# Where ScalarE copies a list's own mask: ahead of the list's other columns, or behind its last evacuation

## The chip, the cores and the metric

The kernel runs on one core of a Trainium2 chip. The metric is the device time of one execution in microseconds (us); where several executions were timed, the median is given. Lower is better.

## The reference, cut to what matters

Four graph attention layers on 4096 nodes with 256 features, each with a residual and a layer norm. All four use one adjacency matrix, which is about 1/256 full and has its diagonal set:

```python
x = layernorm(x + gat0(x, adj, ...))     # 4 heads of 64
x = layernorm(x + gat1(x, adj, ...))     # 4 heads of 64
x = layernorm(x + gat2(x, adj, ...))     # 2 heads of 128
x = layernorm(x + gat3(x, adj, ...))     # 1 head of 256, a positive and a negative softmax
# in each layer, for node i and neighbour j:
#   e_ij = leaky_relu(s_i + d_j, 0.2), -inf where adj_ij is 0
#   out_i = sum_j softmax_j(e_ij) * v_j
```

## The kernel before, in words

**Lists.** The 4096 nodes are 32 row tiles of 128. A row tile of 128 nodes has neighbours in about 40% of all nodes, so the kernel does not run over all columns. For each row tile it packs a *list*: 14 groups of 128 columns each (`NP = 14`), of which 13 are gathered neighbours and one, at place `FRONT = 6`, is the row tile itself. A list has two products. One is the packed mask, `cm`, of 128 x 14 x 132 bytes: for each packed column, 128 mask bytes and four bytes with the digits of the column's node number. It is stored to `maskC` in HBM. The other is the table `idx` of node numbers, which is worked out from the digits and stays on the chip. All four layers read both.

**How a list is made** (`lists`, L288). Four row tiles make a block. For a block, `prepare` (L370) loads raw adjacency (L378, four buffers `raw`), has ScalarE convert it to mask bytes `mk` (L380), and VectorE reduces it to which columns are hit (L384). `places` (L389) works out where each hit column goes in the list. `pack` (L422) then makes one list: VectorE builds one-hot matrices `oh` (L436), TensorE multiplies them with `mk` into PSUM banks (L442), and ScalarE evacuates each full bank into `cm` (L449, five evacuations per list: four of three groups, one of one group). The group `FRONT` needs no matmul: ScalarE copies it from `mk` (L425). When `cm` is whole, SyncE issues its store (L450), and three small VectorE operations make the index table from it (L453 to L455). The pool of `cm` has three buffers (L297), so a list's buffer is the one that the list three before used.

**The layers.** In a layer, each row tile gathers its 13 groups of node rows with indirect DMAs on GpSimd (L634), and loads its own rows (L631), its packed mask (L626) and a row of scores (L624) through SyncE. ScalarE computes weights (L687, 42 per row tile in layer 0), VectorE more weights and the masking (L678, L682, L684, L688), and TensorE multiplies weights and gathered rows (L696). Row tiles are done in two halves of seven groups. The result is normalised on VectorE (L1014 to L1017, L967 to L988), and projected for the next layer: L536 transposes, L541 copies, L550 multiplies, L568 and L574 (ScalarE) with L570 and L576 (VectorE) make the row that L578 stores. L588 and L589 make and store the scores.

**What runs beside what** (`run`, L482). Layer 0 begins before the lists are done. The first ten to fourteen lists are made while layer 0's projections run (up to about 160 us). From then on one list and one conversion step are made between the two halves of each row tile of layer 0, ten row tiles ahead (`LEAD = 10`). The last list is stored at 664 us. From there on layers 0 to 3 run alone. (A dense path behind the packed one runs only where a list overflows, which this input doesn't cause.)

**What sets the order.** The program gives instructions in the order of the code, but a scheduler places them in each engine's queue by its own estimate of when they can start. An engine works through its queue in order. So an instruction that depends on little can be placed a long way ahead of its neighbours in the code; its waits are then met where it stands in the queue. L425 depends on `mk`, which is there for a whole block at a time, and on its buffer.

Of the kernel before, what the change touches and what calls it, by code (L numbers as in the profile page):

```python
# [44 lines left out]
AF = mybir.ActivationFunctionType  # L45
# [33 lines left out]
FRONT = 6  # L79
# [3 lines left out]
EDGE = 64.0  # L83
# [105 lines left out]
class Program:  # L189
# [98 lines left out]
    def lists(self, ctx):  # L288


        tc, nc, ins, shared = self.tc, self.nc, self.ins, self.shared
# [52 lines left out]
        for j in range(NT):  # L344
            m = 0
            while m < NT:
# [3 lines left out]
                e = m  # L350
# [5 lines left out]
                m = e  # L356
# [7 lines left out]
        class Block:  # L364
# [57 lines left out]
            def pack(self, it):  # L422
                m, mk = self.blk * BT + it, self.mk
                cm = cmp_.tile([P, NP, MC], U8, name="cm")
                nc.scalar.copy(cm[:, FRONT, :], mk[:, m, it, :])  # L425
                order = [j for j in range(NT) if j != m]
                touches = {}
                for j in order:
                    a, n = WINDOW[m, j]
                    for k in range(a, a + n):  # L430
                        touches.setdefault(k // 3, []).append((j, k))
                accs = {}
                for j in order:
                    a, n = WINDOW[m, j]
                    oh = ohp.tile([P, WMAX], BF16, name="oh")
                    nc.vector.tensor_scalar(oh[:, :n * P], iota[:, :n * P], self.place[:, it, j:j + 1], None,  # L436
                                            op0=ALU.is_equal)
                    for k in range(a, a + n):
                        b, s = divmod(k, 3)
                        if b not in accs:  # L440
                            accs[b] = prog.bank(prog.pthree)
                        nc.tensor.matmul(accs[b][:, s * MC:(s + 1) * MC], oh[:, (k - a) * P:(k - a + 1) * P],  # L442
                                         mk[:, j, it, :].bitcast(FP8), start=touches[b][0] == (j, k),
                                         stop=touches[b][-1] == (j, k), skip_group_check=True)
                        if touches[b][-1] == (j, k):
                            e = min(3, NG - 3 * b)
                            got = accs[b][:, :e * MC].rearrange("p (s c) -> p s c", c=MC)
                            o = 3 * b + (3 * b >= FRONT)
                            nc.scalar.activation(cm[:, o:o + e, :], got, AF.Copy, scale=EDGE / 2.0)  # L449
                nc.sync.dma_start(out=shared["maskC"][m], in_=cm)  # L450

                t = wk.tile([P, NP], F32, name="t")
                nc.vector.scalar_tensor_tensor(t, cm[:, :, P], 16.0, cm[:, :, P + 1], op0=ALU.mult, op1=ALU.add)  # L453
                nc.vector.scalar_tensor_tensor(t, t, 16.0, cm[:, :, P + 2], op0=ALU.mult, op1=ALU.add)
                nc.vector.tensor_tensor(shared["idx"][:, m, :], t, limit, op=ALU.min)  # L455
# [1034 lines left out]
```

## Time and profile before

| | before |
|---|---|
| median of 3 runs | 2287.78 us (2284.84 to 2289.15) |
| the profiled execution | 2288.18 us, span 2286.40 us |
| busy: TensorE, weight load | 2026.1 us, 1835.8 us |
| busy: VectorE, ScalarE, GpSimd | 1798.3 us, 1741.5 us, 1493.2 us |
| mean granted TensorE clock | 0.961 |
| list copies L425 | 32 of 0.30 us |
| list evacuations L449 | 160, mostly of 0.50 us |
| stores of `cm` L450 | 32, the first at 66.3 us, the last at 664.2 us |

Times in the profile count from the start of the span. "L425" is line 425 of the kernel before. In a view of the chain of work or of waits, a piece such as "DMA maskC<-cm" is the time from the issue of a store to its landing, for which the next piece waited. In a view by stretches, "busy" counts an engine's instructions only, so a stretch's length less an engine's busy time is that engine's idle time. PEclk is the granted TensorE clock as a share of full speed.

### The profile page before, as it was taken

What the parts mean: (1) busy time and instruction counts of PE and PEld (TensorE: products, weight loads), DVE (VectorE), ACT (ScalarE), POOL (GpSimd) and SP (SyncE); (2) the same over time, 40 slices, a digit from 0 to 9 for tenths busy, and PEclk for the clock granted to TensorE, in tenths of its full rate; (3) what the DMA queues carried; (4) which work ended last, traced back from release to release, by engine and by line L of the source; (5) the groups of instructions that cost most, each with busy time, mean ns of one, the idle gap of its engine ahead of it and who ended that gap; (6) DMA issues with size and microseconds to landing.
All of it is one profiled execution on the core that took longest, in us unless ns stands there. A gap on an engine that the chain in (4) does not pass through costs nothing.

```text
span 2286.4 us, 49074 instructions
## 1 busy us (share of the span) xinstructions
PE 2026.1 (89%) x15689; PEld 1835.8 (80%) x15689; DVE 1798.3 (79%) x5317; ACT 1741.5 (76%) x4977; POOL 1493.2 (65%) x1596
## 2 busy tenths in 40 slices
PE   4888888988999968998889898989998799999996
PEld 2667877877889958998888887989997688888885
DVE  2898998989999968998888895887885365566566
ACT  4778887977789958988788886988883666676664
POOL 2117664646567777777777777777761677777773
PEclk7999999999999989999999999999999899999998
DMA  8889777866456765666666666778764788888884
GB/s 279 257 262 349 219 231 250 282 201 212 143 155 188 208 181 158 190 182 165 177 170 172 176 168 176 221 213 233 217 201 139 243 268 274 270 259 282 261 255 139
DMA packets 250320, 493.00 MB, mean 216 GB/s; under 512 B 44385, under 2 KB 156610, under 8 KB 249666
## 3 DMA queue, kind: packets, MB, share of 16 engines
q0 software_dynamic: 81536, 245.30, 38.0%
q1 hardware_dynamic: 168514, 244.46, 33.5%
q8 instruction: 126, 2.06, 0.4%
q14 instruction: 144, 1.18, 0.2%
HBM read 437.05 MB, written 52.54 MB: 214 GB/s over the span
## 4 chain that ended last, share of the span: by engine, by line
PE 51%; DVE 15%; DMA 14%; ACT 11%; issue 5%; POOL 3%; SPq 0%; DVEq 0%; ACTq 0%; POOLq 0%
PE bank L699 16%; PE bank L696 14%; PE bank L938 10%; DMA G<-vals,idx 8%; ACT w L687 6%; PE bank L550 5%; PE bank L442 4%; POOL G L634 3%; DVE w L688 3%; DMA raw<-in_adjB_dram 2%; DVE w L684 2%; DVE oh L436 2%; DVE w L678 1%; DMA G<-vals 1%; ACT mk L380 1%
## 5 line engine op out<-in xcount | busy, mean ns | idle before, releaser
L634 POOL DMA_INDIRECT G<-vals,idx x1456 | 1480.2, 1017 | 754.2 <-issue 205.0
L687 ACT ACTIVATE w<-S,G 128x128 f32<-128x128 f32 x3248 | 988.2, 389 | 122.9 <-DMA G<-vals,idx 106.8
L696 PE MATMUL bank<-w,G 128*65 128x128 f32 x7168 | 842.9, 277 | 102.0 <-DVE w L684 79.0
L696 PEld LDWEIGHTS bank<-w,G 128*65 128x65 f32 x7168 | 800.6, 140 | 120.8 <-DVE w L684 91.3
L699 PE MATMUL bank<-G,w 128*128 128x257 f32 (+1 forms) x2688 | 491.3, 340 | 33.6 <-DVE w L666 11.8
L699 PEld LDWEIGHTS bank<-G,w 128*128 128x128 f32 x2688 | 431.8, 193 | 83.5 <-DVE w L666 14.7
L688 DVE SCALAR_TENSOR_TENSOR w<-w,bank 128x896 f32<-128x896 f32 x384 | 411.7, 1081 | 21.0 <-ACT w L687 20.5
L938 PE MATMUL bank<-vw,pw 128*128 128x129 f32 (+1 forms) x2048 | 301.2, 304 | 6.6 <-issue 3.2
L938 PEld LDWEIGHTS bank<-vw,pw 128*128 128x128 f32 x2048 | 276.9, 193 | 23.7 <-issue 3.7
L664 ACT ACTIVATE w<-S,G 128x128 f32<-128x128 f32 x392 | 140.0, 391 | 128.7 <-DMA G<-vals 64.3
L436 DVE TENSOR_SCALAR oh<-iota,place 128x256 bf16<-128x256 f16 (+2 forms) x992 | 225.7, 304 | 14.7 <-PE bank L442 14.1
L442 PE MATMUL bank<-mk,oh 128*128 128x132 fp8e4 x2336 | 188.5, 224 | 18.1 <-DVE oh L436 9.2
L550 PE MATMUL bank<-wext,xT 128*128 128x268 f32 (+3 forms) x640 | 181.5, 415 | 16.4 <-ACT xT L541 14.4
L678 DVE TENSOR_TENSOR w<-S,G 128x256 f32<-128x256 f32 x384 | 154.4, 418 | 51.8 <-DMA G<-vals,idx 48.9
L442 PEld LDWEIGHTS <-oh 128*128 128x128 bf16 x2336 | 144.2, 98 | 58.8 <-DVE oh L436 27.3
L380 ACT ACTIVATE mk<-raw 128x1024 uint8<-128x1024 int32 x128 | 130.7, 1053 | 25.8 <-DMA raw<-in_adjB_dram 25.7
L550 PEld LDWEIGHTS bank<-wext,xT 128*128 128x128 f32 x640 | 118.4, 203 | 35.6 <-ACT xT L541 16.9
L927 ACT ACTIVATE pw<-Sw,d 128x512 f32<-128x512 f32 x192 | 131.6, 714 | 17.0 <-PE bank L938 12.7
L935 DVE TENSOR_TENSOR pw<-pw,mw 128x512 f32<-128x512 f32 x64 | 44.0, 692 | 124.3 <-ACT pw L934 65.6
L928 DVE SCALAR_TENSOR_TENSOR pw<-pw,mw 128x512 f32<-128x512 f32 x192 | 126.9, 692 | 18.2 <-ACT pw L927 17.4
L684 DVE SCALAR_TENSOR_TENSOR w<-w,bank 128x896 f32<-128x896 f32 x128 | 138.7, 1083 | 0.9
L688 DVE SCALAR_TENSOR_TENSOR w<-w,mk 128x896 f32<-128x896 f32 x80 | 86.7, 1087 | 43.1 <-ACT w L687 42.0
(131 smaller groups left out, 1605.0 us busy)
## 6 DMA issues: line engine op xcount, KB each, us to landing
raw<-in_adjB_dram SPq DMA_DIRECT2D x128, 512.0 KB
mk<-maskC SPq DMA_DIRECT2D x112, 231.0 KB
G<-vals,idx POOLq DMA_INDIRECT x1456
S<-edge SPq DMA_DIRECT2D x64, 256.0 KB
vw<-vals SPq DMA_DIRECT2D x96, 129.0 KB
xp<-y SPq DMA_DIRECT2D x96, 128.0 KB
y<-xp SPq DMA_DIRECT2D x96, 128.0 KB
mw<-maskW SPq DMA_DIRECT2D x20, 528.0 KB
```

The lines of the kernel that those rows point to most:

```text
L380: nc.scalar.activation(mk[:, q:q + 2, :, :P], src, AF.Copy, scale=EDGE)
L436: nc.vector.tensor_scalar(oh[:, :n * P], iota[:, :n * P], self.place[:, it, j:j + 1], None, op0=ALU.is_equal)
L442: nc.tensor.matmul(accs[b][:, s * MC:(s + 1) * MC], oh[:, (k - a) * P:(k - a + 1) * P], mk[:, j, it, :].bitcast(FP8), start=touches[b][0] ...
L550: nc.tensor.matmul(pp[:, :c1 - c0], self.xT[:, k, :], wext[:, k, c0:c1], start=(k == 0), stop=(k == KT - 1 and brow is None))
L634: nc.gpsimd.indirect_dma_start(out=self.place(pos), out_offset=None, in_=sh["v"][n][:NODES[t], :], in_offset=bass.IndirectOffsetOnAxis(ap= ...
L678: nc.vector.tensor_tensor(w[h][:, k:k + 2, :], S[:, h:h + 1, :].to_broadcast([P, 2, P]), dd[:, :, V + T + h:V + T + h + 1].to_broadcast([P ...
L684: nc.vector.scalar_tensor_tensor(w[h], w[h], LEAST, mh, op0=ALU.max, op1=ALU.mult)
L687: nc.scalar.activation(w[h][:, k, :], S[:, h, :], AF.Exp, bias=d(k, h))
L688: nc.vector.scalar_tensor_tensor(w[h], w[h], LEAST, mh, op0=ALU.max, op1=ALU.mult)
L696: nc.tensor.matmul(accs[0][:Wd, h * P:(h + 1) * P], v, w[h][:, k, :], **how)
L699: nc.tensor.matmul(a, w[h][:, k, :], v, **how)
L938: nc.tensor.matmul(accs[it][:, c:c + Wd], p[:, it, :], v[:, c:c + Wd], start=(j == 0 and h == heads[0]), stop=(j == NT - 1), skip_group_ch ...
```

## The change

The copy of a list's own mask is written behind the loop that evacuates the list's banks. `tc.issue_after(last.ins)` gives it one more edge of order, without a semaphore: on ScalarE's queue it must stand behind the list's last evacuation. The copy itself, its engine, its operands and the number of buffers are the same.

```diff
             def pack(self, it):
                 m, mk = self.blk * BT + it, self.mk
                 cm = cmp_.tile([P, NP, MC], U8, name="cm")
-                nc.scalar.copy(cm[:, FRONT, :], mk[:, m, it, :])
                 order = [j for j in range(NT) if j != m]
...
-                            nc.scalar.activation(cm[:, o:o + e, :], got, AF.Copy, scale=EDGE / 2.0)
+                            last = nc.scalar.activation(cm[:, o:o + e, :], got, AF.Copy, scale=EDGE / 2.0)
+
+                with tc.issue_after(last.ins):
+                    nc.scalar.copy(cm[:, FRONT, :], mk[:, m, it, :])
                 nc.sync.dma_start(out=shared["maskC"][m], in_=cm)
```

In the changed kernel the lines L426 to L449 of before have numbers one smaller (the evacuation is L448), the lines from L450 on have numbers two larger (the store is L452), and the copy is L451.

## The prediction

> **What bounds the kernel now.** I first read the page: no engine is idle for long over the whole span, so the answer lies in a stage. Section 4, the chain that ended last, gives the shares:
>
> ```profile
> PE 51%; DVE 15%; DMA 14%; ACT 11%; issue 5%; POOL 3%; SPq 0%; DVEq 0%; ACTq 0%; POOLq 0%
> ```
>
> DMA holds 14% of the chain. To see whether the tile that the change touches is part of that, I asked for everything that writes or reads `cm`:
>
> ```profile
> L449 ACT ACTIVATE cm<-bank x160: 253/501/513, 62.0 to 663.9; 128x396 uint8<-128x396 f32 x128, 128x132 uint8<-128x132 f32 x32
> L425 ACT COPY cm<-mk x32: 283/300/312, 25.7 to 607.4; 128x132 uint8<-128x132 uint8 x32
> ...
> its engine sat idle before it (us, times) until:
> ...
>   DMA maskC<-cm: 23.6, 6
> ```
>
> The 32 copies of L425 run early: the last starts at 607.4, the last evacuation at 663.9. So a list's copy stands in ScalarE's queue far ahead of that list's evacuations. As the list's first writer it must wait for its buffer, which is free once the store of the list three before has landed. Six of these waits cost ScalarE 23.6 us. The chain in order of time, around the first long one:
>
> ```profile
> 362.12 0.27 ACT cm L449
> 362.39 0.03 ACT w L687
> 362.42 6.42 DMA maskC<-cm
> ...
> 368.93 0.30 ACT cm L425
> 369.24 0.01 issue
> 369.24 0.27 ACT row L574
> 369.51 0.02 issue
> 369.54 0.07 DVE row L576
> ```
>
> The store issued at 362.42, right after a list's last evacuation, is waited for by the copy of the list three later, which ScalarE reaches at once. The activation L574 behind the copy is held too, and VectorE's L576 waits for L574. ScalarE's timeline has four such waits, before the copies at 368.93 (5.71), 464.35 (5.92), 559.05 (6.06) and 607.40 (3.31): 21.0 us. A fifth, 2.35 us at 211.72, was followed by 3.25 us for raw adjacency data, which lands late anyway; a sixth is 0.2 us.
>
> What a stall is worth is read from VectorE, which is full in this stage when nothing stalls. Busy time by stretch (length; then PE, weight load, VectorE, ScalarE, GpSimd busy; clock; DMA share; GB/s):
>
> ```profile
> 324.00:348.00 24.00, 21.68 (x217) 19.48 (x215) 23.95 (x73) 24.00 (x72) 15.62 (x16) 1.00 0.87 280
> 348.00:373.50 25.50, 20.55 (x196) 17.66 (x196) 22.03 (x64) 19.55 (x61) 14.81 (x16) 0.97 0.95 334
> 373.50:396.00 22.50, 20.31 (x170) 18.93 (x171) 20.08 (x78) 15.71 (x45) 8.35 (x9) 0.81 0.52 140
> 444.00:469.00 25.00, 20.13 (x197) 17.69 (x198) 21.42 (x66) 16.46 (x57) 16.02 (x18) 0.97 0.81 262
> 469.00:492.00 23.00, 20.66 (x173) 19.24 (x174) 20.43 (x77) 15.52 (x44) 7.81 (x8) 0.81 0.54 153
> 539.00:563.50 24.50, 19.79 (x196) 17.57 (x196) 20.78 (x64) 16.11 (x55) 17.01 (x16) 0.99 0.73 230
> 563.50:587.00 23.50, 21.08 (x188) 19.66 (x189) 22.17 (x85) 14.78 (x51) 7.81 (x8) 0.86 0.41 121
> 608.00:630.00 22.00, 19.89 (x196) 17.49 (x196) 19.68 (x62) 19.02 (x65) 12.42 (x13) 1.00 0.49 135
> 650.00:672.00 22.00, 19.79 (x197) 17.91 (x197) 22.00 (x77) 15.50 (x52) 12.65 (x14) 1.00 0.60 165
> ```
>
> Without a stall (first and last row) VectorE idles 0.05 and 0.00 us. In the others it does, and in the stretch after each of the three long stalls the clock is 0.81 to 0.86.
>
> **What the Trainium skill says.** "Perfetto Trace Analysis", Per-engine timelines: ScalarE and VectorE are strict FIFO. The trace agrees: L574 started 0.31 us after the blocked copy, not before. "DMA: Bandwidth & Descriptors", Anatomy of one DMA: the semaphore fires only when the last byte is confirmed in the target memory, with HBM the heaviest; here SyncE is busy 0.32 us with the store, and it is waited for 6.42. "TensorE: Matmul & The Clock Gate", What's actually happening: an idle window of about 3.4 us halves TensorE's clock, and busy time restores it. The trace agrees: after the first stall TensorE was busy 0.71 of 3 us (369 to 372), then the clock was 0.50 from 372 to 378, and the 56 matmuls of L696 took 8.82 us against 6.33 at full clock.
>
> **The change part by part.**
>
> *Removed: the early copies and their wait.* ScalarE's work is the same: 32 copies of 0.30 us. The buffer's wait passes to the list's first evacuation, which in the changed build's order comes two lists and a half after the store it needs, some 50 us (stores are 20 to 26 us apart) against 6. So the wait costs nothing; without that cover it is at most the 6 us of before. Gain: VectorE's idle time in the stretches of a stall and its aftermath. First: (25.50 - 22.03) + (22.50 - 20.08) = 5.89. Second: (25.00 - 21.42) + (23.00 - 20.43) = 6.15. Third: (24.50 - 20.78) + (23.50 - 22.17) = 5.05. Fourth: 22.00 - 19.68 = 2.32 (587 to 608 was full). Sum 19.4 us. The first halves are the wait for L574 (3.30, 3.57, 3.71 on VectorE's timeline); the second halves are VectorE waiting for list matmuls L442 (2.30, 2.47, 1.23), late because TensorE ran at half clock. What is late next: nothing but VectorE. With the copy gone, L574 could end near 364, and VectorE reaches L576 at 366.2.
>
> *Added: a copy behind the last evacuation.* It costs 0.30 us alone and 0.20 behind another instruction (two of them took 0.50 at 25.72). "ScalarE: Activation LUTs", What ACT_TABLE_LOAD costs, gives 186 + 0.833 x 132 = 296 ns less 93 of overlap: the same. Who waits for it: the store L450, with the loads L624 and L378 behind it in SyncE's queue, and L453 on VectorE, with everything behind that. The store is read back some ten tiles later, so 0.3 us is hidden; SyncE waits for ScalarE here anyway. The gathers on GpSimd use the indices equally late. L453 matters: in 26 of 32 lists it starts within 0.25 us of the last evacuation. The changed order puts one more 1.0 us operation (L688) ahead of it in 12 of these, which covers the copy. It stays bare in 14, ten of them before 162 us. Cost between 0 and 14 x 0.30 = 4.2 us; I take 2.0, since VectorE is not full in the early lists (108 of 160 us).
>
> *Moved: the scheduler's order elsewhere.* Instruction counts are equal on every engine; GpSimd's order is unchanged, and all orders agree from the last list (664 us) on. Conversions L380 slide by a few places. At lists 20, 24 and 28 the five evacuations now stand in one burst ahead of 21 L687, where before they were mixed with them. At list 16 the burst was there already, and VectorE was busy 23.94 of 24 us, so I set it to nothing; the rival below prices it. Below nothing too: another 1.45 + 1.01 us of VectorE's idle time (396 to 421, 492 to 515) might close.
>
> *Sum.* -19.4 + 2.0 = -17.4 us. From the profiled execution's own 2288.18 (span 2286.40) that is 2270.8; the median 2287.78 is 0.4 below it, so **2270.4 us**. All of it reaches the end, since the layers after are fed by this one.
>
> **The rivals.**
> 1. *Only the direct part goes.* If TensorE drops to half clock at these places for another gap, the second halves (2.42 + 2.57 + 1.33) and the fourth stall stay: 19.4 - 6.3 - 2.3 = 10.8, less the whole 4.2: gain 6.6, 2281. For it: a second spell (0.54 from 393 to 396) follows a gap of 2.09 us behind list 20, with no stall of its own. Against: the gap that caused it is the stall's.
> 2. *More than the idle time counted.* VectorE's whole idle time from 200 to 690 is 31.4 us (490 less 458.6 busy); all of it gone is 2256. Half of what I left out is 2264. Against: 5.0 of it waits for raw data at 215.
> 3. *The gain is hidden.* ScalarE, freed earlier, reaches the conversions L380 before their data has landed and waits as long: 2288. For it: 1.50 and 1.06 us of such waits (397, 492). Against: most loads are issued a list ahead.
> 4. *Slower: the bursts.* At lists 20, 24 and 28, 13 of the L687 (0.297 us each) move behind the last evacuation: 3.9 us during which VectorE may have nothing. If TensorE then falls to half clock for two halves (2 x 2.5), a place costs 8.9, three 26.7; less 19.4 it is +7.3, 2295. It decides from 6.5 us a place. Against: list 16; and VectorE has masks, place and norm work there.
>
> **How the numbers follow.** Forecast (2266 to 2275) 0.64; rival 1, 0.13; rival 2, 0.08; rival 3, 0.09; rival 4, 0.06. A measurement here can tell about 0.2% (4.6 us) from no change: 2283.2 is the line. Faster is forecast, rival 2 and rival 1: 0.85; same 0.09, slower 0.06. The range from 2262 to 2282 leaves out rivals 3 and 4 and a part of rival 2, under 0.2.
>
> **What would show it.** Right: no wait of ScalarE for the store of `cm`; that store gone from the chain; VectorE idle under 1 us in the stretches of lists 19 to 28; no half clock after lists 19, 23 and 27; L453 waiting for the copy for some 2 us in all. The step on the bursts is wrong if VectorE waits for L687 after lists 20, 24 and 28; the central step is wrong if ScalarE's 21 us turn up before L380 or L449.

## The result, and the profile after

| | before | after |
|---|---|---|
| median of 6 runs each | 2288.47 us (2284.84 to 2290.04) | 2268.28 us (2262.22 to 2274.81) |
| ratio, 95% interval | | 0.9916 [0.9897, 0.9935] |
| profiled execution, span | 2288.18 us, 2286.40 us | 2271.01 us, 2269.3 us |
| store of list 19, of list 32 | 362.42, 664.21 us | 365.97, 646.65 us |
| from there to the end of the span | 1622.2 us | 1622.7 us |

The kernel is faster by 0.84%, and the interval leaves out 1. The whole of it lies between the stores of lists 19 and 32. Here and below, a ratio and its interval are those of the fast runs; the ratio can differ by up to 0.0014 from the plain quotient of the two medians beside it.

First the tile that the change touches. Everything that writes `cm` in the kernel after, and what ScalarE and VectorE waited for ahead of it (us, times):

```profile
L448 ACT ACTIVATE cm<-bank x160: 268/501/511, 61.4 to 646.2; 128x396 uint8<-128x396 f32 x128, 128x132 uint8<-128x132 f32 x32
L451 ACT COPY cm<-mk x32: 298/302/312, 65.4 to 646.3; 128x132 uint8<-128x132 uint8 x32
...
its engine sat idle before it (us, times) until:
  PE bank L441: 48.0, 54
  ACT cm L451: 3.7, 6
```

The copies now run from 65.4 to 646.3, each right behind its own list's evacuations. The line "DMA maskC<-cm: 23.6, 6" is gone: neither the copy nor the evacuation waits for a store. A new line stands in its place: VectorE waited 3.7 us in six places for the copy (before, 1.6 us in two for the evacuation that then came last).

Then the stretches where the stalls were, shifted to where the same lists are now made (length; then busy time and instructions of PE, weight load, VectorE, ScalarE, GpSimd; clock; DMA share; GB/s):

```profile
366.00:390.00 24.00, 20.35 (x194) 17.55 (x195) 23.96 (x90) 13.98 (x48) 12.91 (x13) 0.99 0.74 237
390.00:411.00 21.00, 20.68 (x200) 19.22 (x199) 20.66 (x62) 20.94 (x62) 11.54 (x11) 0.93 0.64 215
453.00:474.00 21.00, 19.26 (x189) 16.57 (x187) 21.00 (x78) 11.43 (x40) 12.99 (x13) 1.00 0.66 209
474.00:496.00 22.00, 19.02 (x173) 18.65 (x173) 21.76 (x63) 21.65 (x67) 9.76 (x10) 0.84 0.64 205
541.00:562.00 21.00, 19.33 (x189) 16.59 (x187) 21.00 (x79) 10.94 (x35) 12.60 (x12) 1.00 0.66 215
562.00:587.00 25.00, 22.87 (x213) 22.12 (x213) 24.52 (x72) 21.82 (x76) 11.82 (x11) 0.86 0.50 148
587.00:610.00 23.00, 22.29 (x228) 20.78 (x227) 23.00 (x73) 18.02 (x63) 15.51 (x16) 1.00 0.61 177
610.00:630.00 20.00, 19.39 (x203) 17.98 (x201) 20.00 (x63) 16.15 (x55) 12.72 (x13) 1.00 0.54 150
```

VectorE idles 1.1 us in these 177 us (177.00 less 175.90); before, 19.4 us in 166 us. ScalarE, which caused the stalls, idles in plenty (10 of 21 us from 541 to 562). It is not the bound here, and its idle time costs nothing.

The half clock behind lists 19, 23 and 27 is gone: in the rows that begin at 366, 453 and 541 the clock is 0.99 to 1.00. But it fell to half in three other places. The same view, by 3 us:

```profile
390.00:393.00 3.00, 3.00 (x17) 3.00 (x16) 2.81 (x9) 3.00 (x12) 0.00 (x0) 0.51 0.32 117
477.00:480.00 3.00, 2.78 (x13) 2.78 (x14) 2.99 (x8) 3.00 (x12) 0.00 (x0) 0.50 0.73 248
566.00:569.00 3.00, 3.00 (x16) 3.00 (x15) 2.81 (x8) 3.00 (x12) 0.00 (x0) 0.50 0.21 77
```

These are the places behind the bursts of evacuations at lists 20, 24 and 28. ScalarE works through 21 weights L689 (L687 of before) and TensorE has just had a gap (in 474 to 477 it was busy 0.23 of 3 us). Yet VectorE is busy 2.81, 2.99 and 2.81 of 3 us: here it has masks and weights to make and waits for none of the slow matmuls. The bursts are not needed for such spells: the kernel before, where the evacuations were mixed with other work, had one behind each of the same lists (392 to 396, 488 to 491 and 580 to 583 us):

```profile
393.00:396.00 3.00, 3.00 (x17) 3.00 (x16) 2.88 (x8) 2.80 (x5) 0.00 (x0) 0.54 0.82 188
488.00:491.00 3.00, 3.00 (x16) 3.00 (x15) 3.00 (x7) 3.00 (x6) 0.00 (x0) 0.50 0.80 238
580.00:583.00 3.00, 2.78 (x13) 2.79 (x14) 3.00 (x8) 0.75 (x4) 0.00 (x0) 0.52 0.25 85
```

### The profile page after: what moved, and what is told of

It is laid out like the page before. It is cut to its first block, busy times and chain, and to the rows that moved or that the text cites. A ratio compares the mean times of both kernels' runs of the same rounds, so it can differ in the third digit from the quotient of the medians.

```text
span 2269.3 us, 49072 instructions
## 1 busy us (share of the span) xinstructions
PE 2019.7 (89%) x15689; PEld 1834.6 (81%) x15689; DVE 1798.0 (79%) x5317; ACT 1738.5 (77%) x4977; POOL 1494.7 (66%) x1596
## 5 line engine op out<-in xcount | busy, mean ns | idle before, releaser
L689 ACT ACTIVATE w<-S,G 128x128 f32<-128x128 f32 x3248 | 988.2, 389 | 123.0 <-DMA G<-vals,idx 109.1
```

Of the source, the lines that this page charges most:

```text
L689: nc.scalar.activation(w[h][:, k, :], S[:, h, :], AF.Exp, bias=d(k, h))
```

## The experiments

Two kinds of chip came up. On some the kernel before takes 2287 to 2291 us, as above. On two occasions it took 2764.3 and 2798.2 us; in the profiles from there TensorE pauses where nothing shows a releaser (last section). Whether that belongs to the chip or to the occasion the runs do not show. Each run is compared with the kernel before on its own chip.

**E5, the change once more**, to have a second profile (its diff is that of the change).

> The change itself, beside the kernel before on the same chip. In the first four experiments the kernel before took 2764 us, and TensorE's idle time had no releaser in the profile for 230 us before L696: TensorE paused by itself. Where it does so, VectorE isn't the bound of the list stage and a stall of ScalarE has room: the change should be within 0.2% of before. Where the kernel before takes about 2288 us, the change should be 20 us faster, 2268 (2262 to 2275).

Measured: 2268.08 us against 2290.62, ratio 0.9915 [0.9892, 0.9938]; profiled span 2265.1 us. In this profile the chain that ended last could be followed to the start (that of the first one breaks off at 1527 us):

```profile
PE 48%; DVE 19%; DMA 14%; ACT 10%; issue 5%; POOL 3%; SPq 1%; DVEq 0%; ACTq 0%; POOLq 0%
```

Before, four landings of the store of `cm` stood in the chain, at 362.42, 458.46, 553.01 and 602.39, of 6.42, 5.80, 5.93 and 4.92 us: 23.1 us. Now there is none. VectorE's share has grown from 15 to 19%. Behind the store of list 19, at 363.25 here, the chain runs on VectorE:

```profile
364.25 1.00 DVE w L690
365.24 0.10 DVE t L456
365.34 0.33 DVE row L578
365.67 0.08 DVE idx L457
```

L578 (L576 of before), which had waited 3.30 us for ScalarE at this place, follows VectorE's own work.

**E1 and E6, the copy left in front, six buffers in place of three.** Is the stall the cause, or the new order of the queues?

```diff
-        wk, cmp_ = pool("iwk", 2), pool("cm", 3)
+        wk, cmp_ = pool("iwk", 2), pool("cm", 6)
```

> The copy stays where it was, ahead of the list, but the tile cm has six buffers instead of three, so a copy waits for the store of the list six before, which is long landed. If the wait for the buffer is what the change removed: ScalarE no longer waits for a store of cm, and the time is 20 us under before, 2268 (2262 to 2274). If the gain came from the new order of the queues (copy behind the evacuations, conversions moved), it is not there: 2284 to 2291, with other waits in the place of the old ones.

Measured, on the chip of 2764.3 us: 2764.1 us, ratio 1.0003 [0.9987, 1.0019]. The wait for the store was gone here too, and the time did not move. The change with its copy behind for lists 11 to 32 showed no gain on this chip either (E2 below), so E6 is the same kernel on a chip like the first.

> The copy in front with six buffers of cm, as before. Where the kernel before takes about 2288 us: if the wait for the buffer is what was removed, 2268 (2262 to 2274), as the change or a little better, since nothing is added behind the last evacuation; if the new order of the queues made the gain, 2284 to 2291. Where it takes about 2764 us: no difference from before.

Measured: 2269.06 us against 2290.62, ratio 0.9909 [0.9882, 0.9935]. The writers of `cm`, copy in front:

```profile
L425 ACT COPY cm<-mk x32: 283/301/314, 26.0 to 542.0; 128x132 uint8<-128x132 uint8 x32
...
its engine sat idle before it (us, times) until:
  PE bank L442: 42.4, 45
  ACT cm L449: 2.6, 5
```

The copies run as early as ever, up to five lists ahead, and no one waits for a store. From the store of list 19 to that of list 32 it takes 282.3 us; before 301.8, after 280.7. So the gain comes from the buffer's wait and not from the copy's new place as such. (A kernel that keeps the wait and has another order of the queues was not run on this kind of chip.)

**E11 and E12, four and two buffers with the copy in front.** In the built order of the kernel before, the four copies that stalled stand 5, 1, 1 and 2 instructions behind the last evacuation of the list whose buffer they take; the others stand 7 or more behind it, and but one of them (list 15, 14 behind, 2.35 us) waited 0.3 us at most. Is it that distance, or the number of buffers?

```diff
-        wk, cmp_ = pool("iwk", 2), pool("cm", 3)
+        wk, cmp_ = pool("iwk", 2), pool("cm", 4)
```

> The kernel before, copy in front, with four buffers for cm in place of three. In the built order the scheduler then puts the copies up to three lists ahead in place of two: again right behind the last evacuation of the list whose buffer they take. Theory (what counts is the distance on ScalarE's queue between that evacuation and the copy): before, the copies that stalled stood 5, 1, 1 and 2 instructions behind it (lists 22, 26, 30, 32), and those 10 or more behind it did not; with four buffers they stand 7, 6, 1 and 1 behind it for lists 19, 23, 27 and 31. So four waits for the store of cm, 17 to 23 us in all, at one list later each, and no gain or a small one: 2283 to 2292 where before takes 2288. Rival (what counts is the number of buffers: a store lands in 6 us, so one more list of room is enough): no wait, and the whole gain, 2266 to 2270.

```diff
-        wk, cmp_ = pool("iwk", 2), pool("cm", 3)
+        wk, cmp_ = pool("iwk", 2), pool("cm", 2)
```

> The kernel before, copy in front, with two buffers for cm. In the built order the copies of lists 21, 25, 29, 31 and 32 stand 1 to 5 instructions behind the last evacuation of the list two before, those of lists 20, 23, 24, 27 and 28 stand 6 or 7 behind it. Theory of the distance: five waits of about 6 us and five of 3 to 4 us, 40 to 50 us in all where before has 23.6; at the price of before (about 20 us of time for 21 us of waits) 13 to 27 us slower than before: 2300 to 2315 where before takes 2288. Rival (a wait is worth little beyond the four places, since VectorE catches up): within 5 us of before.

Both came to a chip where the kernel before takes 2798.17 us. Times there tell nothing on this point, as with E1: 2803.41 us, ratio 1.0012 [0.9991, 1.0033], and 2801.17 us, 1.0004 [0.9990, 1.0018]. The waits can be read. ScalarE's timeline with four buffers, the copies that waited for a store:

```profile
337.86 0.30 ACT L425 COPY cm<-mk 128x132 uint8<-128x132 uint8 x1 [0.48 <-DMA maskC<-cm]
...
459.52 0.30 ACT L425 COPY cm<-mk 128x132 uint8<-128x132 uint8 x1 [1.76 <-DMA maskC<-cm]
...
579.00 0.30 ACT L425 COPY cm<-mk 128x132 uint8<-128x132 uint8 x1 [3.03 <-DMA maskC<-cm]
...
696.78 0.30 ACT L425 COPY cm<-mk 128x132 uint8<-128x132 uint8 x1 [4.65 <-DMA maskC<-cm]
```

Counted from the first copy, these are the copies of lists 19, 23, 27 and 31: the four that were named, and no other. A fourth buffer took no wait away. The scheduler used it to put the copy a list further ahead, again right behind the store it needs. The four copies stand 7, 6, 1 and 1 instructions behind the evacuation, and the nearer they stand, the longer they waited. Their size was overestimated: 9.9 us in place of 17 to 23. In two places of this profile the store landed sooner (issued 575.99, waited for until 579.00; issued 692.15, until 696.78: 3.0 and 4.6 us, against 4.9 to 6.4 on the first). With three buffers in front for the lists behind the tenth (E3, on a chip of this kind) it was 9.3 us, also in four places. With two buffers it was 12.3 us in seven places, in place of 40 to 50: lists 21, 25, 29, 31 and 32, all five named as certain, at 0.90 to 3.12 us each; of the five named as partial only list 20 (0.83), and one not named (list 11, 0.26). So the place of the stalls is shown; what two or four buffers cost in time on the first kind of chip was not measured.

**E8, the copy behind, two buffers.** Is the moved wait covered?

```diff
-        wk, cmp_ = pool("iwk", 2), pool("cm", 3)
+        wk, cmp_ = pool("iwk", 2), pool("cm", 2)
...
+                with tc.issue_after(last.ins):
+                    nc.scalar.copy(cm[:, FRONT, :], mk[:, m, it, :])
```

> The change with two buffers for cm in place of three. The buffer's wait now falls on a list's first evacuation. If it is covered as the prediction says (the store of the list two before was issued 20 us or more earlier, from the list after the eleventh on, against about 6 us until it lands), no wait of ScalarE for the store of cm behind the eleventh list, and the time of the change within 2 us. In the first eleven lists, stored some 10 us apart, a wait of up to a few us may show. If three buffers are needed by the late copy as well: waits of some 6 us return, and the time goes back toward the kernel before (2285 to 2290).

Measured: 2264.75 us against 2287.1, ratio 0.9908 [0.9889, 0.9928], and no wait of ScalarE for a store of `cm` in any list, the first eleven included. With the copy behind, two buffers do what six do with the copy in front. The third buffer of the changed kernel isn't needed.

**E4 and E7, the late copy made three times.** What does the copy cost behind the last evacuation?

```diff
                 with tc.issue_after(last.ins):
-                    nc.scalar.copy(cm[:, FRONT, :], mk[:, m, it, :])
+                    for _ in range(3):
+                        nc.scalar.copy(cm[:, FRONT, :], mk[:, m, it, :])
```

> As the change, with the copy done three times behind the last evacuation (the same bytes each time), which puts two more copies of 0.2 us between the last evacuation and all that reads cm. My step had 14 lists in which the copy is bare on VectorE: 14 x 0.4 = 5.6 us over the change, 2274 (2270 to 2278). If ScalarE's own time is what counts it is 32 x 0.4 = 12.8 us, 2281. If the copy is hidden nearly everywhere: within 2 us of the change.

Measured, on the chip of 2764.3 us: 2779.12 us, ratio 1.0045 [1.0025, 1.0064]. It is about 12 us slower than the kernel before, where E1, E2 and E3 differ from it by less than 4; the change itself was not run there, so what two more copies add to it is read from E7.

> The change with the copy of a list's own mask made three times in a row behind the last evacuation, so 0.4 to 0.6 us more of ScalarE ahead of each list's store and of VectorE's digits. If the added copy costs what the prediction took (bare in 14 lists, about half of it counted), two more cost 14 x 0.4 x 0.5 = 2.8 us over the change, up to 5.6 if it is bare in all 14: about 2271 to 2274 where the kernel before takes 2290. If the copy is hidden behind VectorE's own work except in the first ten lists, where VectorE is not full, within 2 us of the change. If everything behind a list's last evacuation waits for it in all 32 lists: 32 x 0.4 = 12.8 us, 2281.

Measured: 2274.84 us against 2287.1, ratio 0.9951 [0.9938, 0.9963]. That is 0.0036 above the change's 0.9915, 8 us, by the two intervals some 2 to 14. By the profiles the last list is stored at 650.8 us, against 646.65 and 644.14 in the two profiles of the change: 4.1 and 6.6 us later, of which 3.0 and 5.8 us are there by list 19 already. So two more copies cost 4 to 7 us by the stores, mostly in the early lists. Half of that, 2 to 4 us, is an estimate for one copy; no run shows it (E9). The digits' wait for the copy was only 0.2 us here. From 57 to 210 us VectorE's waits shift among several lines (for rows of layer 0's projections, which ScalarE makes, 9.3 us against 4.2 after the change; for list matmuls 2.7 against 7.3), and the trace names none that holds the cost.

**E2, E3 and E9, one part alone.** The copy behind for some lists and in front for the others.

```diff
+                if m < 10:
+                    nc.scalar.copy(cm[:, FRONT, :], mk[:, m, it, :])
...
+                if not (m < 10):
+                    with tc.issue_after(last.ins):
+                        nc.scalar.copy(cm[:, FRONT, :], mk[:, m, it, :])
```

E3 is the reverse. E2 and E3 ran on the chip of 2764.3 us.

> Lists 1 to 10 have the copy in front as before, lists 11 to 32 behind the last evacuation. The profiled stores of cm stood 3.9 us later than before at list 16 and 17.6 us earlier at list 32, so the gain of 21 us lies behind list 19 and a loss of about 4 us in lists 7 to 10. If both hold, this is faster than the change by the 4 us: 2264 (2259 to 2269). If the early loss was chance of one execution, it equals the change: 2268.

> The other half: lists 1 to 10 have the copy behind the last evacuation, lists 11 to 32 in front. The four stalls stay and the early loss comes: 2292 (2288 to 2296). If the early loss was chance: 2288. If the early part carried any of the gain: below 2284.

Measured: 2767.84 us, ratio 1.0016 [1.0003, 1.0030], and 2765.64 us, 1.0005 [0.9989, 1.0022]. The waits went as expected (none in E2, 9.3 us in E3); the times tell nothing of the gain.

> The copy in front of the evacuations for the first ten lists, as before, and behind the last evacuation for the other 22. If the gain comes from the lists behind the nineteenth alone and the late copy costs something in the first ten (1 to 4 us by the times of the stores), 1 to 4 us faster than the change: 2264 to 2268 where before is 2290. If the early difference is only chance between executions, the time of the change within 2 us. If the whole order of the queues mattered, back toward 2290.

Measured: 2263.62 us against 2287.1, ratio 0.9909 [0.9888, 0.9929]. The late lists alone hold the whole gain: from store 19 to store 32, 280.4 us. Its profile has list 19 stored at 361.9 us, ahead of the change (365.97, 363.25) and of before (362.42). From 57 to 210 us VectorE had done 138.8 us of work, in the change's profile 134.9; TensorE's wait for the row of L576 (matmul L584 of the changed kernel) was 4.8 us against 12.1. That looks like a cost of the late copy in the first ten lists, but E8, which has it in every list, had done 138.2 us of VectorE's work in the same stretch. List 19 was stored at 362.42 (before), 364.50 (E6) and 361.92 us (E9) without the late copy in the early lists, and at 365.97 and 363.25 (the change) and 362.51 us (E8) with it: the two groups overlap. As a time it isn't shown either: 0.9909 and 0.9915 lie within each other's interval. So a cost of one late copy is not shown. E9, E8 and E6 are the lowest ratios that were found, and none of them is clearly below the change.

**E10, the copy behind the list's first evacuation.** Early enough to be no last step, late enough not to stand two lists ahead.

```diff
-                accs = {}
+                accs, first = {}, None
...
+                            first = first or evac
...
+                with tc.issue_after(first.ins):
+                    nc.scalar.copy(cm[:, FRONT, :], mk[:, m, it, :])
```

> The copy behind the list's first evacuation in place of its last: it can no longer stand two lists ahead of its own list, and is not the last step ahead of the store either. If the early place of the copy is the whole of the cause, the gain is all there (2266 to 2270 where before is 2290), with no wait of ScalarE for the store of cm, and no wait of the digits for the copy, which is worth 0 to 3 us over the change. If the copy must stand behind the last evacuation for the gain, near 2290.

Measured: 2273.02 us against 2287.1, ratio 0.9947 [0.9927, 0.9966]. The mechanism was in the main as expected: no wait for a store, the last list stored at 644.3 us (the change: 646.65 and 644.14), the digits waiting 2.5 us in four places for the last evacuation. The time missed the expectation: 0.9947 of 2290 is 2278 us, where 2266 to 2270 was expected. Its six runs (2270.65 to 2274.99 us) all lie above the six of E9 on the same chip (2261.12 to 2267.74), so E10 is slower than E9, by some 9 us. Little of that lies in the list stage: in the profiles list 32 is stored 2.0 us later than in E9 (642.33), though VectorE twice waits 1.2 us for a weight of ScalarE. The stage behind the lists, where the order of the instructions is the same, takes 1624.6 us against 1617.4. Why is open. So two kernels can differ by several microseconds outside the part in which they differ, and a gain is better placed by the times of the stores than by the total alone.

## Why the prediction was right

*Forecast 2270.4 us, range 2262 to 2282; measured 2268.28.* Against the profiled execution's 2288.18 the sum gave -17.4; the profiled execution after is 17.2 lower, that of E5, on another chip, 21.4 lower. From store to store, in us:

| stretch, from the store of one list to that of another | before | after | E5 | gain forecast | gain after, E5 |
|---|---|---|---|---|---|
| up to list 19 | 362.42 | 365.97 | 363.25 | -2.0 | -3.6, -0.8 |
| 19 to 21 (first stall) | 52.88 | 45.76 | 46.10 | 5.89 | 7.1, 6.8 |
| 23 to 25 (second) | 51.76 | 45.97 | 45.61 | 6.15 | 5.8, 6.2 |
| 27 to 29 (third) | 49.38 | 45.77 | 45.64 | 5.05 | 3.6, 3.7 |
| 29 to 31 (fourth) | 42.15 | 39.42 | 39.36 | 2.32 | 2.7, 2.8 |
| 21 to 23, 25 to 27, 31 to 32 | 105.62 | 103.76 | 104.18 | 0 | 1.9, 1.4 |
| list 32 to the end | 1622.2 | 1622.7 | 1621.0 | 0 | -0.5, 1.2 |

*Removed.* Right, in mechanism and size: 21.1 and 20.9 us from store 19 to store 32 against 19.4. The sum is closer than its parts, and that is in part luck: the first place was counted 0.9 to 1.2 us too low, the third 1.4 too high, and the places set to nothing gave 1.4 to 1.9 us, near the 2.5 us (1.45 + 1.01) that the prediction had seen and left out. E6 shows that the wait is the cause. What the prediction did not see is why only four of 32 copies stall: the scheduler puts a copy as early as its buffers let it, and a stall is where it lands right behind the evacuation that ends its buffer's last use (E11).

*The signs.* VectorE idled 1.1 us in the stretches of lists 19 to 28 together and at most 0.5 in one of them, where under 1 was named; the digits waited 3.7 us for the copy, where some 2 was named. The store is gone from ScalarE's waits and from the chain.

*The half clock.* "No half clock after lists 19, 23, 27" held. The spells behind lists 20, 24 and 28 stayed (0.50 and 0.51), and VectorE lost nothing there. E5 has only two of them (0.52 at 387 to 390, 0.54 at 475 to 478, and 1.00 from 559 to 565), and its list stage is no shorter: 280.9 us from store 19 to store 32, against 280.7. Behind the stalls of before, the slow matmuls were followed by list matmuls that VectorE waited for. The price lies in who waits for the matmuls, not in the clock. How the gain divides between the stall and the clock's fall behind it was not tried apart; the table shows the two together.

*The bursts (rival 4).* Set to nothing, and that was right: from 386 to 400 us VectorE waited 0.3 us for L689, and in the whole of 200 to 690 us 7.6 us, of which 6.9 is the one place near 215 where raw adjacency lands late.

*Added.* 2.0 us, of a range from 0 to 4.2. The digits waited 2.1 us more than before (3.7 less 1.6), so the wait was sized rightly. That it costs 2 us of time is not shown: half of E7's difference is 2 to 4 us, with the digits waiting only 0.2 us there, but by list 19 the stores of kernels with and without the late copy overlap (E9).

*Moved.* The conversions were set to nothing, and in this profile that is not quite so. At 119.60 a conversion that had waited 1.42 us for its data stood ahead of L576, and VectorE waited 1.43 us for that row:

```profile
119.60 1.06 ACT L380 ACTIVATE mk<-raw 128x1024 uint8<-128x1024 int32 x1 [1.42 <-DMA raw<-in_adjB_dram]
120.57 0.40 ACT L576 ACTIVATE row<-bank,shift 128x2 f32<-128x2 f32 x2
```

This and the added copy are candidates for the loss of 0.8 to 3.6 us up to list 19. E8, with the same late copy, loses 0.1 us there, so the loss may also be chance of one execution, and that it agrees with the forecast of 2.0 is no proof of it.

*The rivals.* 1 (only the direct part, gain 6.6) fell, since VectorE is full behind the stalls as well. 2 (half of the remaining idle time) fell: 13.3 and 13.5 us (E5) of VectorE's idle time from 200 to 690 remain, 6.9 of them at the raw data. 3 (hidden) fell on this chip: ScalarE waits for raw data 7.3 us in that stretch, against 5.8 before. On the chip of E1 it was true in another form: there VectorE waits for TensorE in the list stage,

```profile
DVE oh L436 <- PE bank L442: 83.8, 72, 6.3
```

83.8 us in 72 places from 200 to 650 us (before, on the first chip, 7.7 us in five). That this covers a stall of ScalarE is argued; the times show that E3, with 9.3 us of waits for the store, was no slower than E2, with none.

## What to carry to other kernels

The first writer of a rotating buffer takes over the wait for the buffer's last reader; if it depends on little else, a scheduler can put it as early as its buffer allows, and where that is right behind the work that ends the buffer's last use, as for four of the 32 copies here, all that stands behind it on its engine waits for a DMA to land. Tie such a step to its own round of work, or give the buffer so many copies that the scheduler can't use them all up; one more may only move the stall (E11). Price a stall by the idle time of the engine that bounds the stage, over the stall and what follows it, and not by the stalled engine's own wait or by the granted clock.

## What the runs showed of the hardware

- On two occasions the same kernel took 2764 and 2798 us in place of 2288. Durations on ScalarE were the same (L687: 388 ns mean in E1, 389 in the kernel before on the first chip), TensorE's L696 a little longer (289 to 291 ns against 277), and TensorE stood idle 187 to 218 us (E1, E11, E12) ahead of L696 with nothing that the profile shows to release it ("issue"): from 200 to 650 us in E1, for one, 34.0 us in 45 pauses, at most 1.2 us each. The mean granted clock was 0.89 against 0.96. What makes the pauses is not known. The kernel with six buffers gained 0.9% on the one kind of chip (E6) and nothing that could be measured on the other (E1).
- "DMA: Bandwidth & Descriptors", Anatomy of one DMA, in the Trainium skill puts the fixed part of a transfer that GpSimd issues at about 2 us, most of it the receipt from the memory written; the store here is issued by SyncE. It moves 231 KB and was waited for 4.9 to 6.4 us from its issue on the first chip, and 3.0 and 4.6 us in E11, there at a DMA share of 0.62 (570 to 580 us) and 0.23 (690 to 698 us). Its landing depends on more than its size, and the share of the DMA engines around it does not put these two in order.
- The stage behind the lists, where the kernels do the same work, took 1617 to 1627 us in the profiles of one kind of chip. So a profile's span can differ by up to 10 us for reasons that do not lie in the lists; the stores' times place a gain that the span alone would not.
